# Moving two of GpSimd's three C-decay products from one half of the step to the other in a Mamba-2 plus ternary-FFN kernel

## The chip, the cores and the metric

The kernel runs on one core of a Trainium2 chip. A core has a matrix engine (PE in the profile; PEld is its weight load), VectorE (DVE), ScalarE (ACT), GpSimd (POOL) and a sync engine whose queue issues DMAs (SP). They run their own instruction streams in order and wait for each other through semaphores. The metric is the device time of one execution in microseconds; before the change the median of three runs is 1155.3 us (1153.39 to 1156.26).

## The reference

The input x has 16 sequences of 512 tokens with 256 features. One layer is computed, in float32:

- x is normalised (layernorm), giving x1. A Mamba-2 block runs on x1: an input projection gives z (512 wide), xBC (512 + 128 + 128 wide) and dt (8 heads); xBC goes through a causal convolution of width 4 and a silu; dt goes through a softplus; then, for every head, a state S of 64 x 128 follows the recurrence

```
S = dA_t * S + (x_t * dt_t) outer B_t        dA_t = exp(dt_t * A)
y_t = S C_t
```

- y gets a skip term D*x, is gated with silu(z), scaled by its root mean square, and projected back to 256 features. The layernorm of (x1 + that) is added to x.
- The result x2 is normalised again, goes through a feed-forward block 256 -> 1024 -> 256 with ternary weights and an exact gelu, and the layernorm of its output is added to x2.

## The kernel before

The recurrence is cut into four chunks of 128 tokens per sequence (NC = 4), and each chunk is done with matmuls. Inside a chunk, a decay matrix mt (128 x 8 heads x 128) times the product of B and C acts on the chunk's own inputs. What earlier chunks left in the state is brought in by a second set of matmuls, `py<-ct,state` (L644), where ct is C times the decay from the chunk's start to each token. Chunk 0 has no earlier state, so ct has three parts, for chunks 1, 2 and 3. The tile ct arrives by DMA with the decays alone (`stage_d`), broadcast over the 128 partitions; `stage_e` multiplies each part in place by C on GpSimd (L499, 128 x 1024 elements each). These three products are what the change moves.

The stages of one sequence, as far as they matter here:

- `stage_a`: input projection and convolution. PE makes a block of projections (`pm`, L296; `pz`, L318), ACT scales and applies silu (`cv` L301, `zs` L322, `xbc` L308), DVE adds the three shifted taps (`cv`, L303).
- `stage_a2`: the softplus of dt, as a chain of small DVE instructions on 128 x 32 elements (L420, L421, L422, L424, L427 to L438). Its result `a` (L438) feeds the matmuls `pd` (L449, L450), which make the sums of the decays.
- `stage_b2`: the scan over the chunks. For each chunk, `prepare` transposes x (`px`, PE), makes `xdt` (DVE L590), B C (`pg`, PE), and `xend` (POOL L603). Then PE makes the chunk's state `pst` (L623); for chunk 0 ACT copies it to SBUF (`state`, L626), and for later ones DVE adds it (L629) to the earlier state, which POOL has decayed (`state`, L651). PE makes `py` (L637, L644), DVE adds the skip term (`y`, L656), POOL multiplies by the gate (`zs`, L660), ACT squares (`y`, L567) and POOL sums the squares (L568, L569).
- `stage_c1`: the output projection (`po`, L709), both norms between the blocks, and the split of the normalised tokens x3 into three bf16 parts, `x3p`: PE transposes x3 into `pt_f` (L735), ACT casts the first part (L738), DVE takes the rest (`rests`, L739), ACT casts the second part (L742), and POOL subtracts it for the third (L743).
- `stage_c2`: the feed-forward matmuls, `ph` (L755) over the three parts of x3p, and `pf` (L789).

The sequences are software-pipelined. A loop over i = 1 to 14 runs two half steps. The first `interleave` holds `stage_a` of sequence i+1 beside `stage_c1` of sequence i-1; the second, here called the scan's half step, holds `stage_b2` of sequence i beside `stage_c2` of i-1 and the decays of i+1. Before the loop a first interleave starts sequences 0 and 1, and after it two more finish sequences 14 and 15.

The order of the instructions on PE, ACT, DVE and POOL is written out by hand (`manual_schedule`): no scheduler rearranges it. Each stage is a generator that yields pieces of work, and `interleave` takes the next piece from the stream whose share of progress, `lo + (hi - lo) * done / work`, is the smallest. The numbers next to a stage in a list are its work, lo and hi. A stage with the place 0.32 to 0.33 therefore puts all its instructions at about a third of its half step. On each engine the instructions then run in exactly the order in which they were emitted.

PSUM tiles come from small rings (`ps_a` four buffers, `ps_tr` two, `ps_c` two), and ct has one buffer.

Of the kernel before, what the change touches and what calls it, by code (L numbers as in the profile page):

```python
# [37 lines left out]
NC = L // P  # L38
# [22 lines left out]
def mamba_ffn_kernel(  # L61
# [18 lines left out]
    NB = x.shape[0]  # L80
# [287 lines left out]
    def stage_a5(b):  # L368

        seqs[b].pop("block")(NCV - 1)  # L370
        yield 1.72

    def stage_a6(b):

        for act in seqs[b].pop("late"):
            act()
        yield 0.1
# [8 lines left out]
    def stage_sil(b):  # L386
        s = seqs[b]
        s["sil"] = small.tile([P, NC * NH], F32, tag="sp_s", name=f"sp_s_{b}", bufs=1)
        nc.scalar.activation(s["sil"], s["neg"], AF.Silu)
        yield 0.1  # L390


    def stage_a0(b):
        norm = Norm(xin[b], f"a{b}")
        norm.stats(0, 1)
        yield 0.2
        norm.stats(2, 3)
        norm.offset(0, NC)
        yield 0.4
        x1 = three.tile([P, NC, DM], F32, tag="x1", name=f"x1_{b}")  # L400
        norm.normal(x1, 0, 1, 2, 3)
        normed[b] = x1
        yield 0.4

    def stage_t0(b):
        x1 = normed[b]
        x1T = one.tile([P, 2, L], F32, tag="x1T", name=f"x1T_{b}")
        transposed(x1T, x1, f"a{b}")
        normed[b] = x1, x1T
        yield 0.9  # L410
# [72 lines left out]
    def stage_d(b):  # L483


        s = seqs[b]
        s["ct"] = one.tile([P, NC - 1, NH, P], F32, tag="ct", name=f"ct_{b}")
        nc.sync.dma_start(
            s["ct"].rearrange("p c h t -> p (c h t)"),
            s.pop("way")[NH:, :].rearrange("w t -> (w t)").partition_broadcast(P),  # L490
        )
        yield 0.1

    def stage_e(b):

        s = seqs[b]
        xbc, ct = s["xbc"], s["ct"]
        for c in range(1, NC):
            nc.gpsimd.tensor_tensor(  # L499
                ct[:, c - 1], ct[:, c - 1],  # L500
                xbc[:, 5, c * P : (c + 1) * P].unsqueeze(1).to_broadcast([P, NH, P]), ALU.mult,
            )
            yield 0.7 if c == 1 else 0.15


    def stage_r(b, *chunks):

        mts = seqs[b].setdefault("mts", [])
        for c in chunks:
            mt = big.tile([P, NH, P], F32, tag="mt", name=f"mt_{b}_{c}")  # L510
            nc.sync.dma_start(
                mt.rearrange("p h t -> p (h t)"),
                seqs[b]["raw"][c * NH : (c + 1) * NH, :].rearrange("h t -> (h t)")
                .partition_broadcast(P),
            )
            mts.append(mt)
            yield 0.1

    def stage_s_v(b, *chunks):

        s = seqs[b]
        for c in chunks:
            mt = s["mts"][c]
            for h in range(NH):
                nc.vector.tensor_scalar(
                    mt[:, h, :], mt[:, h, :], s["cums"][:, c * NH + h : c * NH + h + 1], 0.0,
                    ALU.subtract, ALU.min,
                )
                if h % 2 == 1:
                    yield 0.25  # L530
# [14 lines left out]
    def stage_b1(b, *chunks, sign=-1.0):  # L545

        for c in chunks:
            mt = seqs[b]["mts"][c]
            nc.scalar.activation(mt, mt, AF.Exp, scale=sign)  # L549
            yield 0.1  # L550
# [259 lines left out]
    def chain(*stages):  # L810
        for st in stages:
            yield from st

    def interleave(*streams):


        live = [[g, w, lo, hi, 0.0] for g, w, lo, hi in streams]
        while live:
            at = [lo + (hi - lo) * done / w for _, w, lo, hi, done in live]
            i = at.index(min(at))  # L820
            step = next(live[i][0], None)
            if step is None:
                live.pop(i)
            else:
                live[i][4] += step
# [6 lines left out]
    seqs = {}  # L832
    normed = {}
    endings = []
    E_WORK = 1.0
    A0_WORK, T0_WORK, A_WORK, A2_WORK, B2_WORK = 1.0, 0.9, 18.1, 1.0, 14.9
    C1_WORK, C2_WORK = 1.0, 24.2

# [9 lines left out]
    def run(stage):  # L848
        for _ in stage:
            pass  # L850

    with tc.manual_schedule(engines=ordered):
        interleave(
            (
                chain(stage_a0(0), stage_t0(0), stage_a(0, FIRST, 2)),
                A0_WORK + T0_WORK + A_WORK, 0.0, 1.0,
            ),
            (stage_a0(1), A0_WORK, 0.04, 0.28),
            (chain(stage_sil(0), stage_a2(0)), 0.1 + A2_WORK, 0.42, 0.72),
            (stage_r(0, 0, 1, 2, 3), 0.4, 0.73, 0.74),  # L860
            (scales(1), 3.0, 0.55, 0.8),
        )
        for stage in (
            stage_t0(1), stage_a6(0), stage_s_v(0, 1, 2, 3), ternary(1), stage_s(0, 0), stage_b0(0),
            stage_d(0), stage_b1(0, 0),
        ):
            run(stage)
        interleave(
            (stage_a(1, SECOND), A_WORK, 0.0, 0.8),
            (stage_b1(0, 1, 2, 3, sign=1.0), 0.3, 0.02, 0.03),  # L870
            (stage_b2(0), B2_WORK, 0.1, 0.86),
            (chain(stage_sil(1), stage_a2(1)), 0.1 + A2_WORK, 0.25, 0.47),
            (stage_e(0), E_WORK, 0.3, 0.6),
            (stage_r(1, 0), 0.1, 0.48, 0.481),
            (stage_r(1, 1), 0.1, 0.5, 0.501),
            (stage_a0(2), A0_WORK, 0.5, 0.75),
            (stage_s(1, 0), 1.0, 0.6, 0.65),
            (stage_s(1, 1), 1.0, 0.7, 0.75),
            (stage_r(1, 2), 0.1, 0.66, 0.661),
            (stage_r(1, 3), 0.1, 0.82, 0.821),  # L880
            (stage_t0(2), T0_WORK, 0.81, 0.83),
            (stage_a6(1), 0.1, 0.84, 0.841),
            (stage_b0(1), 0.1, 0.9, 0.901),
            (stage_b1(1, 0, 1), 0.2, 0.902, 0.903),
            (stage_s(1, 2), 1.0, 0.92, 0.95),
            (stage_b1(1, 2), 0.1, 0.96, 0.961),
            (stage_d(1), 0.1, 0.962, 0.963),
        )
        for i in range(1, NB - 1):
            interleave(  # L890
                (ending(), 0.1, 0.0, 0.01),
                *([(chain(scales(2), ternary(2)), 7.0, 0.04, 0.72)] if i == 1 else []),
                *([(stage_a6(i), 0.1, 0.12, 0.13)] if i > 1 else []),
                (stage_a(i + 1, BESIDE, 2), A_WORK - 1.72, 0.0, 1.0),
                (chain(stage_s(i, 3), stage_b1(i, 3)), 1.1, 0.0, 0.01),
                (stage_c1(i - 1), C1_WORK, 0.0, 1.0),
                (stage_e(i), E_WORK, 0.32, 1.0),
            )
            run(stage_a1(i + 1))
            second = [  # L900
                (stage_r(i + 1, 0, 1), 0.2, 0.365, 0.37),
                (stage_s(i + 1, 0), 1.0, 0.44, 0.49),
                (stage_b0(i + 1), 0.1, 0.5, 0.51),
                (stage_b1(i + 1, 0), 0.1, 0.515, 0.52),
                (stage_s(i + 1, 1), 1.0, 0.53, 0.61),
                (stage_b1(i + 1, 1), 0.1, 0.62, 0.63),
                (stage_r(i + 1, 2), 0.1, 0.63, 0.64),
                (stage_s(i + 1, 2), 1.0, 0.72, 0.8),
                (stage_b1(i + 1, 2), 0.1, 0.81, 0.82),
                (stage_r(i + 1, 3), 0.1, 0.82, 0.83),  # L910
            ]
            second.append((stage_c2(i - 1), C2_WORK, 0.02, 1.0))
            second.append((stage_b2(i), B2_WORK, 0.0, 0.98))
            second.append((stage_a2(i + 1), A2_WORK, 0.08, 0.36))
            second.append((stage_a5(i + 1), 1.7, 0.58, 0.66))
            second.append((stage_d(i + 1), 0.1, 0.92, 0.93))
            if i + 2 < NB:
                second.append((stage_a0(i + 2), A0_WORK, 0.6, 0.9))
                second.append((stage_t0(i + 2), T0_WORK, 0.94, 0.97))
            interleave(*second)  # L920
        run(stage_s(NB - 1, 3))
        run(stage_b1(NB - 1, 3))
        run(stage_a6(NB - 1))
        interleave(
            (ending(), 0.1, 0.0, 0.01),
            (stage_c1(NB - 2), C1_WORK, 0.0, 0.235),
            (stage_e(NB - 1), E_WORK, 0.03, 0.16),
            (stage_b2(NB - 1), B2_WORK, -0.02, 0.4),
            (stage_c2(NB - 2), C2_WORK, 0.235, 0.98),
            (stage_c1(NB - 1), C1_WORK, 0.42, 0.9),  # L930
        )
        interleave((ending(), 0.1, 0.05, 0.06), (stage_c2(NB - 1), C2_WORK, 0.0, 1.0))
# [43 lines left out]
```

## Time and profile before

| | |
|---|---|
| median of three runs | 1155.3 us |
| the profiled execution | 1156.0 us |
| its span, first to last instruction | 1154.3 us |
| mean granted PE clock | 0.977 |
| busy: PE | 1090.4 us (94%) |
| busy: DVE | 824.8 us (71%) |
| busy: ACT | 696.4 us (60%) |
| busy: POOL | 588.9 us (51%) |
| `ct` products on POOL (L499) | 48, 113.1 us in all, 2383 ns each |

A "step" below is one turn of the loop; in the trace, from i = 2 on, each takes 67.2 us, and the same instruction comes back 67.2 us later. Times such as 478.88 are microseconds from the start of the span; the examples are mostly from the step whose `ct` products begin at 472.83. In a timeline line the columns are: start in us, duration in us, engine, line, operation, output and inputs with shapes, count, and in brackets how long the engine had been idle before it and what released it. Several equal instructions in a row are merged into one line (`x3`).

### The profile page before, as it was taken

To read this page: it belongs to the slowest core of one execution; us is meant where nothing else is said; L and a number is where in the kernel's file an instruction comes from. 1 tells how busy PE (TensorE), PEld (TensorE's weight loads), DVE (VectorE), ACT (ScalarE), POOL (GpSimd) and SP (SyncE) were. 2 spreads that over 40 slices of the span, in tenths; PEclk is the share of its full clock that TensorE was granted. 3 is DMA by queue.
4 is the path that set the end of the run, shared out by engine and by line. 5 is a ranking of instruction groups with operands and counts; after the bars stand their busy time and mean duration, and the time that the engine had idled before them with its cause. 6 is when DMAs were issued, how large, how long until landed. Compare 5 with 4: busy or idle time off the path is not lost.

```text
span 1154.3 us, 17172 instructions
## 1 busy us (share of the span) xinstructions
PE 1090.4 (94%) x6052; PEld 715.6 (62%) x6052; DVE 824.8 (71%) x2137; ACT 696.4 (60%) x1378; POOL 588.9 (51%) x699
## 2 busy tenths in 40 slices
PE   5787799999999999999999999999999999999897
PEld 2344367575766757576675757667575766757575
DVE  4674867769686776968677695867779586776652
ACT  5628465676666567666656766665675666566321
POOL 1243635646463564646356464635646463565842
PEclk9788899999999999999999999999999999999899
DMA  6312012220312222031222203122220312212000
GB/s 197 124 58 77 18 62 86 74 93 19 130 37 67 82 74 92 19 130 37 70 79 74 93 19 130 37 73 76 74 93 19 130 37 74 75 56 92 1 10 28
DMA packets 34534, 81.23 MB, mean 70 GB/s; under 512 B 4368, under 2 KB 23440, under 8 KB 32400
## 3 DMA queue, kind: packets, MB, share of 16 engines
q1 hardware_dynamic: 32896, 79.97, 20.0%
q8 instruction: 48, 0.79, 0.3%
q10 hardware_dynamic: 1552, 0.16, 0.1%
q14 instruction: 38, 0.31, 0.1%
HBM read 71.21 MB, written 8.91 MB: 69 GB/s over the span
## 4 chain that ended last, share of the span: by engine, by line
PE 56%; POOL 17%; DVE 15%; ACT 9%; issue 2%; DMA 1%; POOLq 0%; ACTq 0%; DVEq 0%
PE pf L789 19%; PE ph L755 12%; POOL ct L499 9%; PE py L637 5%; PE pm L296 5%; DVE cv L303 4%; PE pst L623 4%; ACT mt L538 4%; PE py L644 3%; POOL x3p L743 3%; DVE st_f L224 2%; DVE x L695 2%; ACT mt L549 2%; ACT cv L301 2%; POOL xend L603 1%
## 5 line engine op out<-in xcount | busy, mean ns | idle before, releaser
L303 DVE SCALAR_TENSOR_TENSOR cv<-pm,cw_sb,cv 128x511 f32<-128x511 f32 (+2 forms) x288 | 215.3, 748 | 75.5 <-ACT cv L301 68.3
L789 PE MATMUL pf<-w_sb,hT 128*128 128x256 f32 x1024 | 238.0, 382 | 0.0
L789 PEld LDWEIGHTS pf<-w_sb,hT 128*128 128x128 f32 x1024 | 190.0, 190 | 35.8 <-issue 11.5
L755 PE MATMUL ph<-x3p,w_bf 128*128 128x512 bf16 x768 | 190.5, 382 | 3.1 <-POOL x3p L743 0.7
L296 PE MATMUL pm<-x1T,win_sb 128*128 128x512 f32 x384 | 186.6, 609 | 0.3 <-ACT x1T L276 0.3
L761 ACT ACTIVATE hT<-ph,b_sb 128x512 f32<-128x512 f32 x128 | 88.0, 688 | 130.9 <-PE ph L755 130.7
L538 ACT ACTIVATE mt<-mt,cums 128x128 f32<-128x128 f32 x488 | 152.4, 388 | 0.0
L660 POOL TENSOR_TENSOR zs<-y,zs 128x512 f32<-128x512 f32 x64 | 81.4, 1272 | 108.2 <-DVE y L656 106.5
L709 PE MATMUL po<-wo_sb,zs 128*128 128x256 f32 x512 | 127.0, 393 | 4.1 <-DVE att L715 4.1
L755 PEld LDWEIGHTS <-w_bf 128*128 128x128 bf16 x768 | 70.8, 98 | 88.7 <-issue 24.1
L318 PE MATMUL pz<-x1T,win_sb 128*128 128x512 f32 x256 | 124.9, 611 | 0.7 <-ACT state L626 0.7
L709 PEld LDWEIGHTS po<-wo_sb,zs 128*128 128x128 f32 x512 | 96.9, 194 | 32.5 <-issue 14.3
L296 PEld LDWEIGHTS pm<-x1T,win_sb 128*128 128x128 f32 x384 | 71.1, 193 | 71.9 <-issue 66.1
L499 POOL TENSOR_TENSOR ct<-ct,xbc 128x1024 f32<-128x1024 f32 x48 | 113.1, 2383 | 0.0
L301 ACT ACTIVATE cv<-pm,cw_sb 128x512 f32<-128x512 f32 x96 | 65.1, 678 | 69.1 <-PE pm L296 67.8
L656 DVE SCALAR_TENSOR_TENSOR y<-xbc,dsk,py 128x128 f32<-128x128 f32 x256 | 71.3, 341 | 49.0 <-PE py L644 43.2
L568 POOL TENSOR_TENSOR y<-y 128x256 f32<-128x256 f32 x64 | 46.6, 728 | 115.3 <-ACT y L567 115.3
L637 PE MATMUL py<-mt,xdt 128*64 128x128 f32 x1024 | 95.7, 282 | 0.0
L322 ACT ACTIVATE zs<-pz 128x512 f32<-128x512 f32 x64 | 37.9, 592 | 86.4 <-PE pz L318 86.4
L231 POOL TENSOR_TENSOR rs_c<-rs_c,mhalf 128x2 f32<-128x2 f32 x32 | 25.1, 785 | 125.0 <-DVE rms L579 93.8
L318 PEld LDWEIGHTS pz<-x1T,win_sb 128*128 128x128 f32 x256 | 48.7, 196 | 58.0 <-issue 48.1
L644 PE MATMUL py<-ct,state 128*64 128x128 f32 x768 | 75.6, 276 | 6.9 <-POOL ct L499 6.9
(130 smaller groups left out, 1808.9 us busy)
## 6 DMA issues: line engine op xcount, KB each, us to landing
mt<-raw SPq DMA_DIRECT2D x64, 512.0 KB, 4.0
ct<-way SPq DMA_DIRECT2D x16, 1536.0 KB, 6.3
xin<-in_x SPq DMA_DIRECT2D x16, 512.0 KB, 3.8
out<-o SPq DMA_DIRECT2D x30, 256.0 KB, 2.2
w_in<-in_w SPq DMA_DIRECT2D x1, 1024.0 KB, 8.7
w_sb<-in_w SPq DMA_DIRECT2D x1, 1024.0 KB, 11.0
win_sb<-in_w_in SPq DMA_DIRECT2D x1, 768.0 KB, 6.0
win_sb<-in_w_in SPq DMA_DIRECT2D x1, 512.0 KB, 8.1
```

The costliest lines, as they stand in the source:

```text
L296: nc.tensor.matmul(pm, win_sb[:, k, DI + m * P : DI + (m + 1) * P], x1T[:, k, :], start=(k == 0), stop=(k == 1),)
L301: nc.scalar.activation(cv, pm, AF.Copy, scale=cw_sb[:, m, 3:4])
L303: nc.vector.scalar_tensor_tensor(cv[:, j:], pm[:, 0 : L - j], cw_sb[:, m, 3 - j : 4 - j], cv[:, j:], ALU.mult, ALU.add,)
L318: nc.tensor.matmul(pz, win_sb[:, k, j * P : (j + 1) * P], x1T[:, k, :], start=(k == 0), stop=(k == 1),)
L499: nc.gpsimd.tensor_tensor(ct[:, c - 1], ct[:, c - 1], xbc[:, 5, c * P : (c + 1) * P].unsqueeze(1).to_broadcast([P, NH, P]), ALU.mult,)
L538: nc.scalar.activation(mt[:, h, :], mt[:, h, :], AF.Relu, bias=s["cums"][:, c * NH + h : c * NH + h + 1], scale=-1.0,)
L637: nc.tensor.matmul(py[h % 2 * HD : (h % 2 + 1) * HD, j, :], xdt[:, h * HD : (h + 1) * HD], mts[c][:, h, :], start=True, stop=(c == 0),)
L644: nc.tensor.matmul(py[h % 2 * HD : (h % 2 + 1) * HD, j, :], state[:, h * HD : (h + 1) * HD], ct[:, c - 1, h, :], start=False, stop=True,)
L709: nc.tensor.matmul(po[:, 0:DM], g[:, k, c * P : (c + 1) * P], wo_sb[:, k, :], start=(k == 0), stop=(k == NJ - 1),)
L755: nc.tensor.matmul(ph, w1_bf[:, k, f * P : (f + 1) * P], x3p[:, j, k, :], start=(j == 0 and k == 0), stop=(j == 2 and k == 1),)
L761: nc.scalar.activation(hT[:, f, :], ph, AF.Gelu, bias=b1_sb[:, f : f + 1])
L789: nc.tensor.matmul(pf[:, 0:DM], hT[:, f, c * P : (c + 1) * P], w2_sb[:, f, :], start=(f == 0), stop=(f == NF - 1),)
```

## The change

`stage_e` takes the chunks it is to do as arguments and yields 0.1 after each. In the loop, only the product of chunk 1 stays in the first half step, at the place of the first one before; those of chunks 2 and 3 go into the scan's half step, at 0.34 and 0.48. In the opening and closing interleaves the three products stay in one stream, with equal spacing instead of 0.7 + 0.15 + 0.15.

```diff
-    def stage_e(b):
+    def stage_e(b, *chunks):
...
-        for c in range(1, NC):
+        for c in chunks:
             nc.gpsimd.tensor_tensor(
                 ct[:, c - 1], ct[:, c - 1],
                 xbc[:, 5, c * P : (c + 1) * P].unsqueeze(1).to_broadcast([P, NH, P]), ALU.mult,
             )
-            yield 0.7 if c == 1 else 0.15
+            yield 0.1
...
-            (stage_e(0), E_WORK, 0.3, 0.6),
+            (stage_e(0, 1, 2, 3), 0.3, 0.3, 0.6),
...
-                (stage_e(i), E_WORK, 0.32, 1.0),
+                (stage_e(i, 1), 0.1, 0.32, 0.33),
...
             second.append((stage_d(i + 1), 0.1, 0.92, 0.93))
+            second.append((stage_e(i, 2), 0.1, 0.34, 0.35))
+            second.append((stage_e(i, 3), 0.1, 0.48, 0.49))
...
-            (stage_e(NB - 1), E_WORK, 0.03, 0.16),
+            (stage_e(NB - 1, 1, 2, 3), 0.3, 0.03, 0.16),
```

The instruction streams of the two kernels show what this does: PE, ACT, DVE and SP have the same instructions in the same order, with the same DMAs. On POOL nothing is added or removed; 30 of the 48 products change their place:

- in each of the 14 steps, `ct, ct, ct, x3p, x3p, xend` becomes `ct, x3p, x3p, xend`; the product of chunk 2 stands between `sq` of chunk 0 (L569) and the second decay of the state (`state`, L651), and that of chunk 3 between `zs` of chunk 1 (L660) and the sums of squares of chunk 1 (L568);
- in the opening, the product of chunk 3 moves from behind `off_a` (L237) to directly behind that of chunk 2;
- in the closing, the product of chunk 2 moves from behind `sq` of chunk 0 to ahead of `xend` of chunk 2, and that of chunk 3 from behind `zs` of chunk 1 to the former place of chunk 2's.

More of the change, by code (lines that the diff above doesn't have):

```diff
@@ L834, in mamba_ffn_kernel @@
     endings = []
-    E_WORK = 1.0
     A0_WORK, T0_WORK, A_WORK, A2_WORK, B2_WORK = 1.0, 0.9, 18.1, 1.0, 14.9
```

## The prediction

> **What bounds the kernel now.** I read the page's chain first, then the chain in order of time for one step, then the engines' timelines around the place where it leaves POOL.
>
> ```profile
> PE 56%; POOL 17%; DVE 15%; ACT 9%; issue 2%; DMA 1%; POOLq 0%; ACTq 0%; DVEq 0%
> ...
> L499 POOL TENSOR_TENSOR ct<-ct,xbc 128x1024 f32<-128x1024 f32 x48 | 113.1, 2383 | 0.0
> ```
>
> POOL has 17% of the chain and L499 is its largest part. In order of time, one step:
>
> ```profile
> 472.88 6.99 POOL ct L499 x3
> 479.86 2.24 POOL x3p L743 x2
> 482.10 1.01 POOL xend L603
> 483.16 1.12 PE pst L623 x2
> ```
>
> Taken alone this says: 6.99 us of products stand ahead of x3p and xend, two leave, so 4.6 us per step are saved. The timeline of the same place denies it:
>
> ```profile
> 478.39 0.60 ACT L322 ACTIVATE zs<-pz 128x512 f32<-128x512 f32 x1 [0.36 <-PE pz L318]
> 478.88 0.61 ACT L742 CAST x3p<-rests 128x512 bf16<-128x512 f32 x1
> 479.80 1.18 POOL L743 TENSOR_TENSOR x3p<-rests,x3p 128x512 bf16<-128x512 f32 x1
> 483.16 1.12 PE L623 MATMUL pst<-xend,bT 128*128 128x512 f32 x2 [0.63 <-POOL xend L603]
> ```
>
> The cast that x3p's third part needs ends at 479.49 and stands behind a `zs` that waits for PE itself. The products end at 479.86, only 0.31 us (with the start) after the cast. And PE, in order and packed, stood only 0.63 us for `xend`; its one other gap in the 67.2 us step is 0.14 us (for the cast). So PE bounds a steady step, and a whole step could win no more than 0.77 us, whatever POOL drops.
>
> **Steady steps, i = 2 to 14 (13 of them), the removed products.** x3p then starts as soon as the cast lets it. What that takes the trace shows once for this very instruction, in step 1, where POOL is idle before it: the cast runs 142.21 to 142.85, x3p starts at 142.99, so 143 ns. There it has a second semaphore to wait for; other POOL instructions released by ACT start 77 ns after (`state`: L626 ends 484.90, L651 starts 484.98). The gap shrinks from 311 ns to 143, saving 0.17 us, or to 77, saving 0.23. x3p, xend and pst follow back to back, so PE's 0.63 falls to 0.46 or 0.40. I take 0.17, from the row of the same instruction: 13 x 0.17 = **2.2 us**, if nothing later takes it back; 3.0 at the other end.
>
> **The moved products.** Chunk 2's: after `sq` of chunk 0 (L569 ends 495.18) POOL is idle until L651 at 497.03, which waits for PE's py; 2.37 us in 1.84 us of idle time puts L651 back 0.5 us and `zs` of chunk 1 0.4. Behind L651 stands the DVE addition L629 at 503.62: it has 5 us left. Chunk 3's: POOL is idle 5.84 us before L568 at 505.29; it ends near 501.9. Readers are PE's L644 at 506.2 and 511.75, both far later. ACT's square of chunk 1 at 504.60 does not see `zs` 0.4 us late. No DMA moves; `ct<-way` (513.53) waits for the last py, as before. Cost **0**; the cover is POOL's idle time, and without it L629 would pay only past 5 us.
>
> Rule against it: the Trainium skill, "SBUF — State Buffer", section Who interferes with whom, says that GpSimd and a DVE instruction with two SBUF inputs lock each other out of a shared port pair for a whole instruction, and that issue order decides. The trace shows it, and where it does not bite:
>
> ```profile
> 484.79 0.19 DVE L420 SCALAR_TENSOR_TENSOR sp_z<-sp_n,sp_s 128x32 f32<-128x32 f32 x1
> 484.98 1.04 POOL L651 TENSOR_TENSOR state<-state,dec 128x512 f32<-128x512 f32 x1 [0.65 <-ACT state L626]
> 485.39 0.68 DVE L422 TENSOR_TENSOR sp_z<-sp_z,sp_s 128x32 f32<-128x32 f32 x1
> ...
> 148.93 1.04 POOL L651 TENSOR_TENSOR state<-state,dec 128x512 f32<-128x512 f32 x1 [1.24 <-ACT state L626]
> 148.98 1.04 DVE L424 TENSOR_TENSOR sp_e<-sp_z 128x32 f32<-128x32 f32 x1
> ```
>
> L422 takes 0.19 us when free and 0.68 behind L651; L424 (0.19) takes 1.04. Beside the moved products (495 to 502) DVE runs only L629, L463, L656, L590, L597, L606, each with one operand in PSUM; L303 of that kind took 748 ns beside `ct` as elsewhere. By the rule and the rows the products block nothing. But the earlier xend brings `pst`, ACT's L626 and so L651 forward by the 0.17 or 0.23 us saved, towards L420, which does not move (DVE is packed from 472.3 on). L651 now starts 173 to 199 ns after L420 in the 13 steps. With 0.17 it stays behind by 5 to 30 ns, DVE keeps the port, the chain to `a` (L438) is late by nothing, and 2.2 us stand. With 0.23 it is 36 to 72 ns ahead, and L424's row shows a DVE instruction blocked by an L651 only 50 ns ahead of it; one 3 ns ahead of a DVE instruction (L569 and L429 at 76.01) gave way itself. This is the first rival. The rule alone, "first wins", puts the border at 0, the rows between 3 and 50 ns: by the rule the sum is -2.2 us at 143 ns and the rival's at 77, and the rows say the same.
>
> **Step 1.** Here DVE makes the ternary weights beside the products, with two SBUF inputs:
>
> ```profile
> 134.06 7.64 POOL L499 TENSOR_TENSOR ct<-ct,xbc 128x1024 f32<-128x1024 f32 x3
> 136.57 2.92 DVE L206 SCALAR_TENSOR_TENSOR w_sb<-w_sb,thalf,low 128x512 f32<-128x512 f32 x1
> 139.58 1.07 ACT L738 CAST x3p<-pt_f 128x512 bf16<-128x512 f32 x2 [8.20 <-DVE w_sb L206]
> 140.94 0.80 PE L594 MATMUL pg<-xbc 128*128 128x128 f32 x2 [5.64 <-DVE rests L739]
> ```
>
> The last L206 (0.74 us when free) waits until the second product ends (138.94) and ends 0.55 us after it, at 139.49; ACT, `rests` and PE, idle 5.64 us, follow. With one product, which ends at 136.64, it ends at 137.19: **2.3 us**. The clock: the Trainium skill, "TensorE: Matmul & The Clock Gate", section What's actually happening, has PE at half clock after an idle window of about 3.4 us. The trace has it: L594 took 0.80 us for two against 0.39 elsewhere. The new gap, 3.34 us, is below that, so by the rule the half-clock stretch (141 to 146.5, some 2.8 us of lost work) may go, for at most 5.1 us in all. The rows are less kind: granted clock was 0.83 over 96 to 106, where the longest PE gap is 2.21 us; and with PE warm, xend (ends 146.26) holds pst, at 147.21 now, to 0.9 us. I take 0.2 of it: **2.5 us**.
>
> **Opening.**
>
> ```profile
> 90.96 2.35 POOL L499 TENSOR_TENSOR ct<-ct,xbc 128x1024 f32<-128x1024 f32 x1
> 93.37 0.44 PE L644 MATMUL py<-ct,state 128*64 128x128 f32 x4 [2.51 <-POOL ct L499]
> 97.13 0.69 ACT L301 ACTIVATE cv<-pm,cw_sb 128x512 f32<-128x512 f32 x1 [0.49 <-PE pm L296]
> 100.12 0.83 PE L575 MATMUL pss<-ones,sq 128*128 128x1 f32 x6 [2.21 <-ACT x1T L276]
> ```
>
> The product, now at 83.3 to 85.7, frees PE's 2.51 us, but PE then waits longer at L575 for ACT, which is packed from 89 to 115 except for 0.49 us waiting for PE. That is what is won: **0.5 us**. What stands behind it on POOL (L568) starts 0.3 us later, in 3 us of idle time.
>
> **Closing.** POOL runs packed from 1077.6 to 1092 and has the same instructions up to x3p, which PE awaits (0.74 us at 1089.98): same end. xend of chunk 2 is 2.4 us later (1081.95), before pst at 1082.89; the decay L651 and `zs` are 2.4 us later, L629 then ends near 1087.2, ahead of py at 1090.3, ACT's square and table load end near 1089.7, ahead of `hT` at 1090.40. **0**, with 0.7 us the thinnest cover.
>
> **Sum.** Profiled execution 1156.0 (span 1154.3 and 1.7 around it): -2.2 - 2.5 - 0.5 = -5.2, so 1150.8; it is 0.7 above the median, so against the median 1155.3: **1150.1 us**.
>
> **Rivals.**
> 1. *GpSimd takes the port ahead of L420 (slower or level).* For it: 77 ns is the commoner release, and L424's row. L651 starts near 484.75, ends 485.79; L420 ends 485.84, then L421 and L422 (now free) by 486.45 instead of 486.07: 0.38 us late. `a`, at 490.07 before, is there at 490.45; PE, which now starts `pd` (L449) at 490.33 without a wait, would want it at 490.10 and starts it at 490.51, plus 0.1 us for a weight load no longer hidden (the first pst matmul after its wait took 0.70 us, the next 0.59): 0.28 us later than before. 13 x 0.28 = +3.6, with -3.0 from step 1 and opening: 1155.9, slower by a hair. It decides where the lost port costs PE more than 0.23 us per step. Upper bound: if L422 keeps its own 0.49 us block as well, 0.77 per step, +10 - 3: 1162.
> 2. *The steady steps give nothing*: the saved 0.17 us is eaten by `pd` (its weights load at 490.23, `a` ends 490.07) or by ACT. Only -3.0: 1152.3.
> 3. *The change does what the chain says*, 4.6 us x 13 = 60 us: against it, the cast at 479.49 and PE's 0.63. No chance worth naming.
>
> **How the numbers follow.** Forecast 0.50; rival 1 at its price 0.26, at its bound 0.14; rival 2 0.10. Forecast's own range 1148.3 (77 ns saved and the port kept, 0.9 us less) to 1151.6. Within 0.3% (3.5 us; about what a measurement here tells from no change) lie rival 2 and rival 1 at its price: rounded for edges, faster 0.51, same 0.33, slower 0.16. Range 1148 to 1157.5: it leaves out rival 1's bound.
>
> **What would show it.** x3p released by ACT's L742 with POOL idle some 4 us before it; PE's gap at L623 0.40 to 0.46; L206 at about 1.3 us and PE's gap at L594 about 3.3; no gap at L644 in the opening. Wrong if L420 takes about 1.05 us and PE waits at L449 for L438, or if L623's gap stays at 0.63.

## The result, and the profile after

The change made the kernel slower by 0.4%: median 1158.8 us against 1154.4 us (12 runs each), ratio 1.0041 with a 95% interval of 1.0029 to 1.0054. The forecast of 1150.1 us was wrong, and its range, which ended at 1157.5, did not hold the result. The profiled execution took 1158.1 us, its span 1156.4 us.

The chain that ended last, by engine, is the first thing that looks different in the changed kernel's page:

```profile
PE 48%; DVE 33%; ACT 10%; POOL 4%; issue 3%; DMA 1%; POOLq 0%; ACTq 0%; DVEq 0%
```

POOL, which had 17% of the chain, has 4%; DVE, which had 15%, has 33%. What POOL gave up, DVE took over, and the place where it did so is the one that the first rival named. The timeline of the changed kernel in the same step (start in us, duration in us, engine, line, operation, and in brackets the idle time before and its releaser):

```profile
479.33 2.27 POOL L743 TENSOR_TENSOR x3p<-rests,x3p 128x512 bf16<-128x512 f32 x2 [4.38 <-ACT x3p L742]
482.66 1.12 PE L623 MATMUL pst<-xend,bT 128*128 128x512 f32 x2 [0.40 <-POOL xend L603]
484.49 1.04 POOL L651 TENSOR_TENSOR state<-state,dec 128x512 f32<-128x512 f32 x1 [0.41 <-ACT state L626]
484.53 1.04 DVE L420 SCALAR_TENSOR_TENSOR sp_z<-sp_n,sp_s 128x32 f32<-128x32 f32 x1
486.00 0.19 DVE L422 TENSOR_TENSOR sp_z<-sp_z,sp_s 128x32 f32<-128x32 f32 x1
490.24 0.41 PE L449 MATMUL pd<-a,after 128*128 128x32 f32 x2 [0.24 <-DVE a L438]
```

In the kernel before, `pd` started without a wait:

```profile
490.33 0.31 PE L449 MATMUL pd<-a,after 128*128 128x32 f32 x2
```

Read the changed kernel's lines from the top. `x3p` now waits for ACT's cast, with POOL idle 4.38 us before it, as forecast. PE's wait at `pst` has shrunk from 0.63 to 0.40 us. ACT's copy and POOL's decay L651 follow, and L651 now starts 0.04 us *ahead* of DVE's L420, which therefore takes 1.04 us instead of 0.19: it ends 0.05 us after L651. L422, which used to stand behind L651, is free. The end of the softplus chain is late, and PE has a wait that it did not have: 0.24 us at `pd`, for `a`.

Counted from start to start, `pd` follows the matmul ahead of it by 0.52 us instead of 0.11, and the second `pd` matmul follows the first by 0.13 us instead of 0.03: 0.51 us lost, against 0.23 won at `pst`, which leaves a loss of 0.28 us. All 13 steps from i = 2 on show it; the group of L420 (shortest, median and longest of its 16 executions in ns) in the changed kernel:

```profile
L420 DVE SCALAR_TENSOR_TENSOR sp_z<-sp_n,sp_s x16: 183/1042/1051, 26.2 to 1024.3; 128x32 f32<-128x32 f32 x16
```

A step takes 67.48 us instead of 67.20 (the distance of the same `po` matmul in consecutive steps). Over the 13 steps i = 2 to 14 that is 13 x 0.272 = 3.5 us.

The moved products themselves lie where they were meant to, one behind the other with no gap on POOL:

```profile
495.15 2.36 POOL L499 TENSOR_TENSOR ct<-ct,xbc 128x1024 f32<-128x1024 f32 x1
497.45 1.05 POOL L651 TENSOR_TENSOR state<-state,dec 128x512 f32<-128x512 f32 x1
```

Step 1 went the forecast way. The last L206 takes 0.74 us instead of 2.92, and PE's gap falls from 5.64 to 3.64 us:

```profile
136.53 0.74 DVE L206 SCALAR_TENSOR_TENSOR w_sb<-w_sb,thalf,low 128x512 f32<-128x512 f32 x1
...
138.73 0.49 PE L594 MATMUL pg<-xbc 128*128 128x128 f32 x2 [3.64 <-DVE rests L739]
```

The opening did not. The gap at L644 is gone, but there are two longer ones further on, at L575 (2.21 us before) and at the last group of `po` (2.13 us before):

```profile
98.92 1.44 PE L575 MATMUL pss<-ones,sq 128*128 128x1 f32 x6 [3.75 <-ACT x1T L276]
...
116.83 3.78 PE L709 MATMUL po<-wo_sb,zs 128*128 128x256 f32 x8 [3.78 <-DVE att L715]
```

The same eight `po` matmuls in the kernel before:

```profile
118.02 2.62 PE L709 MATMUL po<-wo_sb,zs 128*128 128x256 f32 x8 [2.13 <-DVE att L715]
```

### The profile page after: what moved, and what is told of

It reads as the page before. It is cut to its first block, busy times and chain, and to the rows that moved or that the text cites. A ratio compares the mean times of both kernels' runs of the same rounds, so it can differ in the third digit from the quotient of the medians.

```text
span 1156.4 us, 17141 instructions
## 1 busy us (share of the span) xinstructions
PE 1091.0 (94%) x6007; PEld 716.0 (62%) x6052; DVE 827.4 (72%) x2137; ACT 695.9 (60%) x1378; POOL 586.8 (51%) x699
## 4 chain that ended last, share of the span: by engine, by line
PE 48%; DVE 33%; ACT 10%; POOL 4%; issue 3%; DMA 1%; POOLq 0%; ACTq 0%; DVEq 0%
PE pf L789 19%; DVE cv L303 9%; PE ph L755 7%; PE pm L296 5%; PE py L637 4%; ACT mt L538 4%; PE py L644 3%; DVE mt L606 3%; PE pst L623 2%; ACT cv L301 2%; DVE st_f L224 2%; DVE x L695 2%; ACT mt L549 2%; DVE rests L739 2%; DVE xdt L590 1%
## 5 line engine op out<-in xcount | busy, mean ns | idle before, releaser
L755 PE MATMUL ph<-x3p,w_bf 128*128 128x512 bf16 x723 | 186.0, 384 | 6.0 <-ACT x3p L742 0.6
L660 POOL TENSOR_TENSOR zs<-y,zs 128x512 f32<-128x512 f32 x64 | 81.3, 1271 | 115.0 <-DVE y L656 114.9
L656 DVE SCALAR_TENSOR_TENSOR y<-xbc,dsk,py 128x128 f32<-128x128 f32 x256 | 71.3, 341 | 45.8 <-PE py L644 39.5
L568 POOL TENSOR_TENSOR y<-y 128x256 f32<-128x256 f32 x64 | 46.5, 726 | 81.2 <-ACT y L567 81.2
L644 PE MATMUL py<-ct,state 128*64 128x128 f32 x768 | 75.6, 276 | 4.4 <-POOL ct L499 4.4
```

Source lines behind the costliest of these rows:

```text
L644: nc.tensor.matmul(py[h % 2 * HD : (h % 2 + 1) * HD, j, :], state[:, h * HD : (h + 1) * HD], ct[:, c - 1, h, :], start=False, stop=True,)
L755: nc.tensor.matmul(ph, w1_bf[:, k, f * P : (f + 1) * P], x3p[:, j, k, :], start=(j == 0 and k == 0), stop=(j == 2 and k == 1),)
```

## The experiments

The theory after the result: L651 reaches the port that POOL and DVE share some 40 ns ahead of L420, L420 waits until L651 ends, and PE pays for it at `pd`; the moved products cost nothing. The main rival: the moved products delay something, on POOL, on ACT, or on DVE's side, and L420 is only a symptom. The second question is where the 3.0 us of opening and step 1 went. In what follows "step" is the distance of the same `po` matmul in consecutive steps of the trace, and every ratio is against the kernel before.

### The port order put back (e1_small_first)

```diff
                 decayed = sb.tile([P, DI], F32, tag="state", name=f"state_{b}_{c + 1}")
+                if c == 0:
+                    nc.gpsimd.tensor_tensor(
+                        s["tiny"], nstate[:, 0:8], nstate[:, 0:8], ALU.add
+                    )
                 nc.gpsimd.tensor_tensor(
```

> The changed kernel with one GpSimd addition of 8 columns (about 0.2 us) ahead of the first state decay of each sequence, reading the state that ACT has just copied, so that the decay (L651 of the changed kernel) reaches the port some 0.15 us after VectorE's first softplus instruction instead of 0.05 us before it. Port theory: that instruction is back at 0.19 us, the third one at 0.5 to 0.7 us, and the step falls from 67.48 us to 67.0 to 67.15 us, in all 4 to 6 us less than the changed kernel, so level with the kernel before or up to 0.2% faster. Moved-products theory (the two products cost time where they stand now): the step stays at 67.48 us or grows.

Measured: ratio 0.9977 (0.9965 to 0.9988), step 67.02. This is the changed kernel with one added POOL instruction of 0.20 us, and it is faster than the kernel before. Its timeline:

```profile
480.68 0.20 POOL L653 TENSOR_TENSOR tiny<-state 128x8 f32<-128x8 f32 x1 [0.41 <-ACT state L627]
480.72 0.20 DVE L420 SCALAR_TENSOR_TENSOR sp_z<-sp_n,sp_s 128x32 f32<-128x32 f32 x1
480.84 1.04 POOL L656 TENSOR_TENSOR state<-state,dec 128x512 f32<-128x512 f32 x1
481.35 0.58 DVE L422 TENSOR_TENSOR sp_z<-sp_z,sp_s 128x32 f32<-128x32 f32 x1
```

The decay (here L656) starts 103 to 131 ns behind L420 in the 13 steps, L420 takes 0.20 us, L422 pays 0.58 as it used to, and PE has no wait at `pd`. Its wait at `pst` stays 0.40. So the shorter wait at `pst` is a real gain, and the order at L420 is what turned it into a loss.

### The moved products with x3p as late as before (e2_fillers)

Two more products, of ct with ones, are added where those of chunks 2 and 3 used to be.

```diff
+    def fillers(b, *chunks):
+        ct = seqs[b]["ct"]
+        for c in chunks:
+            nc.gpsimd.tensor_tensor(
+                ct[:, c - 1], ct[:, c - 1],
+                ones.unsqueeze(1).to_broadcast([P, NH, P]), ALU.mult,
+            )
+            yield 0.1
...
-                (stage_e(i, 1), 0.1, 0.32, 0.33),
+                (chain(stage_e(i, 1), fillers(i, 2, 3)), 0.3, 0.32, 1.0),
```

> The changed kernel, and in the first half step, where the two moved products stood, two products of the same size that multiply the same parts of ct by one: GpSimd's third part of x3p is as late as before, and the moved products also run in their new places. Port theory: the step is 67.20 us, as before the change, first softplus instruction 0.19 us, PE waits 0.63 us at pst and nowhere for the decays' sums. Moved-products theory: the step is 67.48 us or longer, since the products still stand in the scan.

Measured: ratio 1.0002 (0.9991 to 1.0013), step 67.20, PE's wait at `pst` 0.63, none at `pd`, L420 at 0.18 us. The products in their new place cost nothing as long as `x3p` keeps its time, with POOL even fuller than in either kernel. The prediction's cost of 0 for them stands.

### The moved products left out (e3_left_out)

The products of chunks 2 and 3 are left out in the loop's 14 steps; those parts of ct keep the bare decays.

```diff
-            second.append((stage_e(i, 2), 0.1, 0.34, 0.35))
-            second.append((stage_e(i, 3), 0.1, 0.48, 0.49))
```

> The changed kernel without the products of chunks 2 and 3 in sequences 1 to 14: C is left out of those two parts of ct, so two of the four chunks of these sequences are computed with the decays alone. Port theory: as the changed kernel, step 67.48 us, first softplus instruction 1.04 us, time within 0.2% of the changed kernel (0.3 to 0.5% slower than the kernel before). Moved-products theory: the step falls to 66.95 to 67.05 us, and the time to 0.2 to 0.4% below the kernel before.

Measured: ratio 1.0036 (1.0024 to 1.0048), step 67.48. The loss is all there without a single moved product:

```profile
482.63 1.04 POOL L651 TENSOR_TENSOR state<-state,dec 128x512 f32<-128x512 f32 x1 [0.41 <-ACT state L626]
482.67 1.05 DVE L420 SCALAR_TENSOR_TENSOR sp_z<-sp_n,sp_s 128x32 f32<-128x32 f32 x1
...
488.39 0.41 PE L449 MATMUL pd<-a,after 128*128 128x32 f32 x2 [0.25 <-DVE a L438]
```

With e2 this is the pair that settles it: place without earlier `x3p` costs nothing, earlier `x3p` without the products costs everything.

### One product moved instead of two (e11_one_moved)

```diff
-                (stage_e(i, 1), 0.1, 0.32, 0.33),
+                (stage_e(i, 1, 2), 0.2, 0.32, 0.7),
...
-            second.append((stage_e(i, 2), 0.1, 0.34, 0.35))
```

> The changed kernel with the product of chunk 2 back in its old place in the steps, directly behind that of chunk 1; only chunk 3's is moved. Port theory: with two products ahead of it x3p still finds POOL idle (they end near 477.5, the cast at 479.49), so it starts as early as with one, L651 is again 30 to 60 ns ahead of L420, L420 takes 1.04 us, step 67.48 us, ratio about 1.003 to 1.004: the loss does not depend on how much is moved. Rival (the loss is the moved products' own cost beside DVE or ACT): half of it, step 67.34.

Measured: ratio 1.0039 (1.0028 to 1.0051), step 67.47.

```profile
475.04 2.28 POOL L743 TENSOR_TENSOR x3p<-rests,x3p 128x512 bf16<-128x512 f32 x2 [2.05 <-ACT x3p L742]
...
480.19 1.04 POOL L651 TENSOR_TENSOR state<-state,dec 128x512 f32<-128x512 f32 x1 [0.42 <-ACT state L626]
480.23 1.06 DVE L420 SCALAR_TENSOR_TENSOR sp_z<-sp_n,sp_s 128x32 f32<-128x32 f32 x1
```

POOL is idle 2.05 us before `x3p` instead of 4.38, but the step and the order at L420 are the same: once `x3p` is released by the cast, more free time ahead of it is worth nothing. The size of what is moved does not enter the loss.

### DVE's chain moved ahead (e5_softplus_early, e7_before_softplus)

```diff
-            second.append((stage_a2(i + 1), A2_WORK, 0.08, 0.36))
+            second.append((stage_a2(i + 1), A2_WORK, 0.03, 0.381))
```

This puts L420 ahead of L651 by about 3 us, in the changed kernel (e5) and in the kernel before (e7).

> The changed kernel with the softplus chain of dt moved forward in VectorE's order, so that its first four instructions stand ahead of the second chunk's xdt instead of behind its decay matrix (place 0.03 to 0.381 instead of 0.08 to 0.36); the other engines' orders are the same. Port theory: no instruction of the chain meets the state decay, PE waits 0.40 us at pst and not for the sums of the decays, step 66.97 us, so 6 to 7 us less than the changed kernel and 0.1 to 0.3% faster than the kernel before. Moved-products theory: the step stays at 67.4 us or more.

> The kernel before with the softplus chain moved forward on VectorE as in the run with the early softplus, the products where they stood. Port theory: the 0.49 us for which the state decay holds up the chain's third instruction before the change lay in slack, so the step stays at 67.20 us and the time within 0.1%: the early softplus is worth something only once the decay comes earlier. Other theory (the early softplus gains by itself): step 67.10 us, as with the moved products.

Measured: e5 0.9971 (0.9959 to 0.9982), step 67.10; e7 1.0013 (1.0004 to 1.0022), step 67.34. The direction of e5 is right, and the edit alone (e7) does not explain it, since it makes the kernel before slower. But both steps are longer than expected by about the same, 0.13 and 0.14 us. In e7:

```profile
482.50 1.04 POOL L603 TENSOR_TENSOR xend<-xdt,dec 128x512 f32<-128x512 f32 x1
482.98 0.61 DVE L420 SCALAR_TENSOR_TENSOR sp_z<-sp_n,sp_s 128x32 f32<-128x32 f32 x1
...
490.56 0.19 DVE L438 TENSOR_TENSOR a<-dt,negA 128x32 f32<-128x32 f32 x1
490.81 0.41 PE L449 MATMUL pd<-a,after 128*128 128x32 f32 x2
```

L420 now stands behind another POOL instruction, `xend`, and `a` comes at 490.76, 0.05 us before `pd`, where the kernel before had 0.26 us. The first `pd` matmul takes 297 ns instead of 195, and the second starts 133 ns behind it instead of 31. The first one itself stands some 0.03 us later behind the matmul ahead of it. Together that is 0.13 to 0.14 us, the whole difference. e5 shows the same 297 ns. A chain that is late by less than any wait that one sees in a list of waits can still cost 0.1 us.

### The one-off parts (e4_first_step, e8_step1_only, e9_opening_only, e10_closing_only)

e4 has the change in the opening, step 1 and the closing, and leaves steps 2 to 14 as before; the other three have it in one place each. The core of e4 (against the changed kernel):

```diff
-                (stage_e(i, 1), 0.1, 0.32, 0.33),
+                (stage_e(i, *((1,) if i == 1 else (1, 2, 3))), 0.3, 0.32, 0.7),
...
-            second.append((stage_e(i, 2), 0.1, 0.34, 0.35))
-            second.append((stage_e(i, 3), 0.1, 0.48, 0.49))
+            if i == 1:
+                second.append((stage_e(i, 2), 0.1, 0.34, 0.35))
+                second.append((stage_e(i, 3), 0.1, 0.48, 0.49))
```

The edits of the other three, in the kernel before: e8 has the `if i == 1` part of this diff; e9 and e10 call the stage with a flag that makes it yield 0.1 each time:

```diff
-            (stage_e(0), E_WORK, 0.3, 0.6),
+            (stage_e(0, True), 0.3, 0.3, 0.6),
```

```diff
-            (stage_e(NB - 1), E_WORK, 0.03, 0.16),
+            (stage_e(NB - 1, True), 0.3, 0.03, 0.16),
```

> The change in the opening, in step 1 and in the closing alone; steps 2 to 14 have the three products where they stood before. What the prediction gave for these parts: -3.0 us (0.26% faster than the kernel before). What the profiles of the changed kernel and of the runs so far give: the opening costs 0.5 to 0.7 us instead of winning 0.5, since PE stays at half clock for two windows instead of one, and step 1 wins 1.3 to 3.0 us by where the clock's windows fall, so -0.6 to -2.5 us. What the measured times of the changed kernel give, less 13 x 0.27 us for the steady steps: +0.7 us, so no gain at all. Step 67.20 us by every theory.

> The kernel before with the products of chunks 2 and 3 moved in step 1 alone. Prediction: -2.5 us. By the profiles so far: the last ternary weight instruction 0.74 us instead of 2.92, PE's wait at pg 3.3 to 3.8 us instead of 5.6, and -1.3 to -3.0 us (0.11 to 0.26% faster). If the time is level with the kernel before, the gain of 2 us seen at pg is given back later.

> Only the opening's order of the products is that of the change (product of chunk 3 directly behind that of chunk 2); steps, step 1 and closing are as before. Clock theory: PE's wait moves from L644 to L575 and grows there from 2.2 to about 3.7 us, so that a second stretch at half clock follows; from the first py<-ct to the first L206 the opening takes 54.7 to 54.9 us instead of 54.2; ratio 1.0004 to 1.0006. The prediction's sum: 53.7 us, ratio 0.9996. Step 67.20 us in both.

> Only the closing's order of the products is that of the change. All the one-off parts together measured +0.5 us, step 1 alone -1.4, which leaves some +1.9 for opening and closing; the traces give the opening 0.6 of that. The prediction: the closing costs nothing; from the first output projection of the last loop step to the end 93.2 us as before, ratio 1.0000. Rival: it costs the missing 1.3 us, 94.5 us, ratio 1.0011. Step 67.20 us in both.

| | ratio | interval | us |
|---|---|---|---|
| all three (e4) | 1.0005 | 0.9994 to 1.0015 | +0.6 |
| step 1 (e8) | 0.9988 | 0.9979 to 0.9997 | -1.4 |
| opening (e9) | 1.0007 | 0.9997 to 1.0018 | +0.8 |
| closing (e10) | 1.0002 | 0.9989 to 1.0014 | +0.2 |

The us column is the ratio, less 1, times 1154.6. Together the one-off parts are nothing that can be measured, where the prediction had -3.0.

The opening's part is seen in the traces. From the first `py<-ct` to the first L206 it takes 54.16 to 54.22 us in the five traces with the old order (before, e7, e8, e10, e12) and 54.67 to 54.90 in the nine with the new one. In e9 the last group of `po` starts 42.19 us after that first `py`, against 42.72 in the kernel before: the forecast 0.5 us is won up to there. Then it is lost. The granted clock over just these eight matmuls, in the kernel before and then in e9 (stretch and its length in us, busy time and count of PE, PEld, DVE, ACT and POOL, granted PE clock, DMA share, GB/s):

```profile
118.02:120.66 2.64, 2.64 (x10) 2.25 (x11) 1.82 (x7) 0.00 (x0) 1.39 (x3) 0.73 0.00 0
```

```profile
118.17:121.96 3.79, 3.79 (x10) 3.07 (x11) 1.82 (x7) 0.00 (x0) 1.39 (x3) 0.50 0.00 0
```

PE did its earlier work sooner, waited 3.78 us instead of 2.13 ahead of this group, and got half clock for all of it instead of a part: 1.15 us more. 1.15 - 0.53 = 0.62 us, the difference between the two openings.

Step 1, from there to the `po` of the next step, is 0.98 us (e8) and 1.28 us (the changed kernel) shorter than the 57.22 us before, but 2.8 to 3.2 us shorter in e1, e3, e4, e5 and e6. The difference is one stretch at half clock: 6.8 us long in the former, 3.4 us in the latter, after PE gaps of 3.35 and 3.64 us in the former and of 3.68 to 3.79 in the latter. So a longer gap is not what makes the longer stretch. What goes with it, in step 1 of all 14 traces, is PE's idle time (the stretch less PE's busy time) in the first 3.4 us of half clock: 0.08 to 0.46 us where full clock returns after it, 0.63 to 1.80 us where the stretch goes on. This is no rule for other places: in the closing of the changed kernel 0.17 us was followed by the long stretch. The cause stays open. In e8 part of that idle time is a wait that the kernel before does not have:

```profile
140.24 1.10 PE L755 MATMUL ph<-x3p,w_bf 128*128 128x512 bf16 x2 [0.92 <-ACT x3p L742]
```

PE's gap ahead of `pg` falls by the forecast 2.3 us there (5.64 to 3.35), and 0.92 us of it is paid back at once for ACT's cast.

The closing takes 93.20 us in e10 and 93.23 in the kernel before, as forecast. In e3, e4 and e8 it takes 94.8 to 95.1 us, with an additional half-clock stretch near 1090; e8 has the old order there, so the change's order isn't the cause.

### ACT's casts ahead (e12_casts_only, e6_casts_first)

```diff
             nc.vector.tensor_sub(rests[:, k, :], pt, x3p[:, 0, k, :])
-        yield 0.12
+        yield 0.1
```

This puts the casts L742 ahead of the `zs` that they stood behind. e12 is the kernel before with this alone (and the products' stream ending at 0.9 instead of 1.0, which keeps POOL's order in the loop). e6 is the changed kernel with it, with e5's edit, and with the whole softplus chain emitted ahead of the first `y`:

```diff
             nc.vector.scalar_tensor_tensor(acc, acc, k, e, ALU.add, ALU.mult)
-        yield 0.15
+        yield 0.05
...
-        yield 0.25
+        yield 0.35
         yield from sums_of(b, a)
```

> The kernel before, with ACT's two casts for the second part of x3p (L742) ahead of the last zs (L322) instead of behind it; the three products stay where they were. Theory: the casts are ready earlier, but the three products still hold POOL until 479.86, so pst's wait of 0.63 us stays, and only PE's 0.14 us wait of ph for the cast goes: step 67.06 us, ratio 0.998 to 0.9985. Rival: the casts alone are the gain that they brought on top of the moved products (0.48 us per step): step 66.72, ratio 0.9946.

> The changed kernel with the whole softplus chain ahead of VectorE's y of chunk 0, and ACT's two casts of x3p ahead of the last zs of the first half step instead of behind it. If PE is the bound of a step and its only waits left are the 0.40 us at pst and 0.14 us at ph, both behind the cast that waited for PE: both go, step 66.3 to 66.5 us, 10 to 12 us less than the kernel before (0.9 to 1.1% faster). If the cast was not what held x3p once the products were gone: step 66.9 to 67.1 us.

Measured: e12 0.9995 (0.9986 to 1.0005), step 67.20; e6 0.9922 (0.9906 to 0.9938), step 66.62, median 1145.4 us. e12 missed too: I expected 67.06. PE's 0.14 us wait for the cast is gone, but what follows is set by the chain of POOL, from the products through `x3p` and `xend` to `pst`, and PE waits a little longer for that:

```profile
480.74 0.38 PE L755 MATMUL ph<-x3p,w_bf 128*128 128x512 bf16 x1 [0.32 <-POOL x3p L743]
...
481.74 1.12 PE L623 MATMUL pst<-xend,bT 128*128 128x512 f32 x2 [0.62 <-POOL xend L603]
```

In e6 the same edit pays, because the products no longer stand there. PE's wait at `pst` is below 0.1 us, L420 is not blocked, and `a` comes long before `pd`; a new wait of 0.27 us appears at `ph`:

```profile
477.85 1.12 PE L623 MATMUL pst<-xend,bT 128*128 128x512 f32 x2
478.25 0.18 DVE L420 SCALAR_TENSOR_TENSOR sp_z<-sp_n,sp_s 128x32 f32<-128x32 f32 x1
...
479.67 1.46 PE L755 MATMUL ph<-x3p,w_bf 128*128 128x512 bf16 x6 [0.27 <-ACT hT L761]
...
483.52 0.19 DVE L438 TENSOR_TENSOR a<-dt,negA 128x32 f32<-128x32 f32 x1
485.45 0.31 PE L449 MATMUL pd<-a,after 128*128 128x32 f32 x2
```

This version is 0.8% faster than the kernel before, and about 1.2% faster than the changed one. Of the 0.77 us per step that the prediction called the most a step could win, it takes 0.58. What it gains over e5, 0.48 us per step, belongs to the casts and the wholly early softplus together; no run parts them.

## Why the prediction was wrong

**What bounds the kernel** was right. The chain's reading (60 us) was rightly thrown out, PE bounds the step, and e6 won less than the 0.77 us named as its limit.

**The step that failed is the choice of 143 ns** for the release of `x3p`, "from the row of the same instruction". That row is step 1's, where the instruction waits for two semaphores, as the prediction itself says; in the trace of the kernel before it waits for one, ACT's, in every later step. The changed kernel shows 142 ns there again and 76 to 77 ns in every later step, where only the cast is late: the value that the prediction had as the other end. The 66 ns between them look small as a time, and were costed as one (0.17 or 0.23 us). But they decide an order: with the one L651 is behind L420, with the other ahead. The text had worked out just that (36 to 72 ns ahead; measured 39 to 56), and still gave the branch 0.40 against 0.50. Its margin at 143 ns was thinner than the 5 to 30 ns that it named: `x3p`'s gap varies from 310 to 339 ns between the steps, and taken step by step, as for the 36 to 72, the same sum gives 6 ns ahead to 30 behind. A row of the same instruction under other waits was the farther row; the one of another POOL instruction under the same single wait was the nearer.

**The first rival** is what happened, at its price. Its +0.28 us per step was made of L420 blocked, L422 freed, `pd` 0.18 us later and a first matmul 0.1 us longer. Measured: +0.272 per step, L420 at 1042 ns, L422 at 192, PE's wait 0.24 us at L449, the first `pd` matmul 297 ns instead of 195. Its total, +0.6 us, was still 4 us too low, because it took over the -3.0 us of step 1 and the opening. Its upper bound (L422 blocked as well, 0.77) did not occur.

**The port rule** of the Trainium skill ("SBUF — State Buffer", section Who interferes with whom: the first to issue has the shared pair for the whole instruction) stands in every run. L651 26 to 56 ns ahead of L420 (the changed kernel, e3, e11) blocks it for about 0.86 us in all 39 steps; 103 ns or more behind (before, e1, e2), it never does. In step 1 of e3 and e4 L651 starts 0 and 3 ns behind L420: L420 keeps its 185 ns, and L651 takes 1.09 us instead of 1.04. The border, put between 3 and 50 ns in the prediction, lies between 3 ns ahead (a pair of other instructions in the kernel before) and 26 ns ahead.

**The moved products** cost 0, as said (e2, e3).

**Step 1** was right in kind: L206 is free (0.74 us, where 1.3 was expected), PE's gap 3.64 us (3.34 expected). The 2.5 us measured -1.4 us (-2.4 to -0.3) by e8's runs; the traces give -1.0 to -3.2, by whether the second half-clock stretch goes. That stretch was weighed, but only as a part to be won, and the wait for the second cast, 0.92 us in e8 and 0.63 in the changed kernel, was not in the sum.

**The opening** had the wrong sign: -0.5 predicted, +0.5 to +0.7 in nine traces. The step at fault is that the waits were followed to ACT, and PE's clock was not. The text wrote "PE then waits longer at L575" without asking what the longer waits, there and at `po`, do to the clock, although it had weighed the clock for step 1 one paragraph earlier. The rule that it used there, from the Trainium skill ("TensorE: Matmul & The Clock Gate", section What's actually happening: half clock after an idle window of about 3.4 us), does not hold in these traces: in the kernel before, half-clock stretches of 3.4 us begin at 102.2, 112.4 and 119.2 us, behind 3.4 us in which PE was idle for only 1.35, 1.93 and 2.13 us. So `po` met half clock in the kernel before as well. There it set in 1.2 us after the eight matmuls had started (118.02); in the changed kernel, whose wait was longer, it set in at 115.4 us, 1.4 us before they started.

**The closing** cost 0, as said (e10).

**The sum.** Ratio 1.0041 is +4.7 us (3.3 to 6.2). The steps are 3.5 of it, shown. For the one-off parts this leaves +1.2 (-0.2 to +2.7), and the direct measurement of the same parts, e4, has +0.6 (-0.7 to +1.7): the two agree, and no finer split can be had from these runs. Of the 9.9 us between the -5.2 that was forecast and +4.7, the order at L420 thus makes 5.7 (from -2.2 to +3.5), and step 1 and the opening some 4 (from -3.0 to between +0.6 and +1.2). The lower end of the forecast's own range, 1148.3, does not follow from the reason given for it: 0.8 or 0.9 us less than 1150.1 is about 1149.3. The profiles' spans do not help here: the time of the first `py<-ct` alone varies from 69.4 to 76.0 us between the traces.

## What to carry to other kernels

Before an instruction on GpSimd is brought forward, list which DVE instructions with two SBUF inputs start close to it and to all that it releases. Where a forecast shift is as large as such a distance (here 0.17 or 0.23 us against 0.17 to 0.20), the order decides, and tens of ns in the release time must be taken from a row with the same waits. A gain on a waiting engine is only worth what the next wait leaves: here it was 0.23 us per step won at `pst` and 0.50 given back at `pd`, and a 0.2 us filler at the right place turned a loss of 0.4% into a gain of 0.2%. And a wait on PE that disappears can make the next one longer, so compare the granted clock behind the later waits too.

## What was not expected of the hardware

- The price of a late operand has a first part ahead of any visible wait: with `a` ready 0.05 us before `pd` instead of 0.26, the first matmul takes 297 ns instead of 195, in e5 and e7 alike. In e1, with 0.10 us, it takes 241 to 256.
- The blocking has no fixed price: L420 ends 41 to 51 ns after the GpSimd instruction that it stands behind, in all 78 such steps, whether that is L651 (the changed kernel, e3, e11), `xend` (e5, e7) or the addition on 8 columns in e1. That addition also starts ahead of L420, by 27 to 56 ns, but it ends 146 to 175 ns after L420's start, so that L420, which takes 185 ns when free, loses only some 16.
- Past the first 60 us, stretches at half clock came in lengths of 3.4 and 6.8 us, except for the one that the end of the run cuts. In step 1 a PE gap of 3.35 us was followed by the long one and gaps of 3.68 to 3.79 us by the short one, so that the gap's length alone does not foretell the cost.
